# Relative attention on one core: pairs of half heads in another order, with operands loaded in pieces and half of the output inside the loop

## The chip, the cores and the metric

The kernel runs on one core of a Trainium2 chip. The metric is the device time of one execution in microseconds. A core has five engines with an instruction stream each: TensorE (PE; its weight loads are listed as PEld), VectorE (DVE), ScalarE (ACT), GpSimd (POOL) and SyncE (SP), which in this kernel issues every DMA. Instructions of one engine run in order; across engines they wait for semaphores.

## The reference

Two branches over x (16 sequences, 512 positions, 128 features) are added. One is attention with relative positions, 16 heads of 8 features; the other is a feed-forward net with weights of plus or minus one.

```python
xn = (x - mu) / jnp.sqrt(var + 1e-05) * ln_g + ln_b
q = (xn @ Wq + bq).reshape(B, S, H, dh)        # k and v alike
p = (pe @ Wp).reshape(S, H, dh)
content = jnp.einsum('bihd,bjhd->bhij', q + u_bias, k)
pos = _relative_shift(jnp.einsum('bihd,jhd->bhij', q + v_bias, p))
attn = jax.nn.softmax((content + pos) * scale, axis=-1)
head = jnp.einsum('bhij,bjhd->bihd', attn, v).reshape(B, S, Dm)
return head @ Wo + bo                          # the attention branch
...
h = jnp.concatenate([x, -x], axis=-1)
h = s0 * _conn_dense(k0, h)
h = jax.nn.relu(h) * 2
h = s1 * _conn_dense(k1, h)
```

The relative shift makes the position score of row i and column j depend on their distance. The last axis of the scores has 512 columns, so 16 x 16 x 512 rows are normalised.

## The kernel before

**Setup.** Layer norm, projections and the feed-forward branch come first. They leave in DRAM the queries (`qu_scr`, `qv_scr`), keys (`k_scr`), windows of position projections (`p_scr`, `pd_scr`), values (`v_scr`) and the finished residual of both biases and the feed-forward branch (`res_scr`). The first maximum of the attention loop starts 267.95 us after the span's start.

**The loop.** A unit is a group of query rows for one head, over all 16 sequences: 32 units a head, 512 in all. A cycle works on two units, after a fixed list of steps (`STEPS`, yielded by `attention_order`). For a unit, `scores` (L786 to L833) makes the scores in two halves on PE (steps A and B: L797 from the keys, L813 and L826 from the windows), `max_first` (L840, step F) and `max_second` (L845, G and H) reduce over chunks on DVE, `transposed` (L850, T) and `max_over_rows` (L854, N) finish the maximum, and `exponentials` (L859 on PE, L869 on ACT, steps X and Y) writes the exponentials. A pair is 16 units, that is one half of a head's query blocks (`up` 0 or 1): eight cycles. The exponentials of one pair stay in one of two buffers `e_t`, and while the next pair is scored, step V (`weighted`, L887 on PE, L896 copies on ACT) multiplies them with the values; a ninth row of the values gives the denominators. Each of the eight V steps of a pair, k = 0 to 7, makes an eighth of it.

The orders of PE, DVE and ACT are written by hand (`ORDERED`); the order of SP is the scheduler's, until a point near the end from which it is by hand as well. A DMA has to wait for the one eight before it, because eight semaphore lanes are used in turn.

**Loads.** Before, pair n is head n // 2, half n % 2. The keys, windows and values of a head are double-buffered by head (`load_head`, L196 to L208, 13 DMAs), the queries by groups of eight units (`load_queries`, L210 to L228, 12 DMAs of 64 KB), all issued at the second unit of a group.

**Numerators and denominators.** When half of a pair's sums have been copied (`av`), `stored_sums` issues the load of the denominators into a tile of 128x16 (`den`, L921, 8 KB) and four stores of the sums (L926). Later a list of due steps runs at step F of an even unit: the reciprocal (L929) and the store of the inverse (L931); when both halves of a head are there, `divided` loads the numerators (`raw`, L942) and the inverse broadcast to all eight features (`rden`, L943), multiplies on POOL (L946, 128x512) and stores to `head_scr` (L947).

**The tail.** In the last two pairs `last_steps` gathers all heads from `head_scr` into two SBUF tiles `sums` (L960), loads the residual (L970, eight DMAs of 512 KB in all) and divides the last head (L963, L978 on POOL, 8x2048). The last pair's sums are divided in place by `last_sums` (L901 to L909; reciprocal L906, product L907) and moved (L911). Then `output_of` does the output projection for both halves: 64 matmuls (L986), 16 adds of 128x512 (L994) and stores of 256 KB (L997).

Of the kernel before, what the change touches and what calls it, by code (L numbers as in the profile page):

```python
# [44 lines left out]
OTHERS = ((slice(0, L0), slice(0, L0)), (slice(L1, P), slice(L0, P - DH)))  # L45
ORDER = (*OTHERS, (slice(L0, L1), slice(P - DH, P)))
# [41 lines left out]
def rel_attention_and_binary_ffn(  # L88
# [59 lines left out]
    sum_scr = scr("sum_scr", [H - 1, DH, B, 2, 2 * P], F32)  # L148
    rden_scr = scr("rden_scr", [H, B, 2, 2 * P], F32)
    head_scr = scr("head_scr", [P - DH, B, 2, 2 * P], F32)  # L150
# [45 lines left out]
    def load_head(h):  # L196
        m = h % 2
        src = p_scr.rearrange("t (d h) s j -> (t d) h s j", h=H)[:, h]
        src_d = pd_scr.rearrange("t (d h) s n j -> (t d) h s n j", h=H)[:, h]
        for n in range(4):  # L200
            rows_n = slice(32 * n, 32 * n + 32)
            nc.sync.dma_start(
                k_t[m][rows_n], k_scr.rearrange("t (d h) b j -> (t d) h b j", h=H)[:, h, n::4, :]
            )
            nc.sync.dma_start(win[m][rows_n], src[:, :, 3 - n : 3 - n + WIN])
            r, side = n // 2, n % 2
            nc.sync.dma_start(win_d[m][rows_n], src_d[:, side, :, 1 - r : 1 - r + WIND])
        nc.sync.dma_start(v_t[m], v_scr[:, h].rearrange("p b f -> p (b f)"))  # L208

    def load_queries(h, l):  # L210
# [3 lines left out]
        for n in range(4):  # L214
# [15 lines left out]
    with ExitStack() as pre:  # L230
# [515 lines left out]
        stores = [lambda: quads_stored(0), lambda: load_head(0), lambda: load_queries(0, 0)]  # L746
# [35 lines left out]
    with ExitStack() as att:  # L782
        manual = ExitStack()
        manual.enter_context(tc.manual_schedule(engines=ORDERED))
        def scores(n, half, st):

            h, u = st["h"], st["u"]
            sp = st["ps"][half]
            blocks = sp.rearrange("p c a r b -> p (c a) r b")
            kt = k_t[h % 2]  # L790
# [15 lines left out]
            for side, off, dist in ((0, LO_OFF, range(-1, -NC, -1)), (1, UP_OFF, range(1, NC))):  # L806
                for d in dist:
                    cs = [c for c in (2 * half, 2 * half + 1) if 0 <= c - d < NC]
                    if not cs:
# [5 lines left out]
                        lhsT=win[h % 2][:, side, y0 : y0 + P],  # L815
# [8 lines left out]
            for t in range(2):  # L824
# [3 lines left out]
                    lhsT=win_d[h % 2][:, t, UP_OFF - 4 * u : WIND - 4 * u],  # L828
# [9 lines left out]
        def max_first(n, st):  # L838
            st["m"] = wk.tile([P, 2 * P], BF16, tag="m", name=f"m_{n}", bufs=3)
            nc.vector.tensor_reduce(  # L840
                st["m"], flat(st["ps"][0]).rearrange("p c x -> p x c"), AX.X, ALU.max
            )

        def max_second(n, st, c):
            nc.vector.tensor_tensor(st["m"], flat(st["ps"][1])[:, c], st["m"], ALU.max)  # L845

        def transposed(n, st):
            st["pt"] = t_t[:, 0]
            for f in range(2):
                nc.tensor.transpose(st["pt"][:, f, :], st["m"][:, f * P : (f + 1) * P], ident_b)  # L850
# [25 lines left out]
        def weighted(pair, k):  # L876

            h = pair["h"]
# [5 lines left out]
            for r in range(4):  # L884
# [4 lines left out]
                    lhsT=v_t[h % 2][:, v0 : v0 + VW],  # L889
                    rhs=pair["eT"][:, b, c],  # L890
                    start=(c == 0 and (g == 0 or at_end)),
# [8 lines left out]

        def last_sums(pair, half, g):  # L901

            av = pair[half][:, g]
            nc.tensor.matmul(t_bank[:, g], lhsT=sel, rhs=av, start=True, stop=True)  # L904
            inv = sequences(e_t[0], 1, 1)[:, 2 * half + g]
            nc.vector.reciprocal(inv, t_bank[:, g])  # L906
            nc.vector.tensor_tensor(av, av, inv, ALU.mult)  # L907
            if g and half == 0:
                last_moved(pair, half, range(4))  # L909

        def last_moved(pair, half, rs):  # L911
            for r in rs:
                b = 8 * half + 2 * r
                nc.sync.dma_start(sums[1][L0:L1, b : b + 2], pair[half][32 * r : 32 * r + DH])

        def stored_sums(pair, half):
# [6 lines left out]
            for r in range(4):  # L923
                b = 8 * half + 2 * r
                dst = sum_scr[h, :, b : b + 2, up, :] if h < H - 1 else sums[up][L0:L1, b : b + 2]
                nc.sync.dma_start(dst, av[32 * r : 32 * r + DH])  # L926

            def inverted():
                nc.vector.reciprocal(den, den)  # L929
                inv = rden_scr[h, bs, up]  # L930
                nc.sync.dma_start(inv.rearrange("b (q m) -> b q m", q=16), den)  # L931
                if h == H - 1:
                    load_rden(half)
                elif up == 1 and half == 1:
                    divided(h)
# [3 lines left out]
        def divided(h):  # L939

            raw, rden = (wk.tile([P, S], F32, tag=name, name=f"{name}_{h}", bufs=1) for name in ("raw", "rden"))
            nc.sync.dma_start(raw, sum_scr[h].rearrange("w b u i -> (w b) (u i)"))  # L942
            nc.sync.dma_start(  # L943
                rden, rden_scr[h].rearrange("b u i -> b (u i)").unsqueeze(0).to_broadcast([DH, B, S])
            )
            nc.gpsimd.tensor_tensor(raw, raw, rden, ALU.mult)  # L946
            nc.sync.dma_start(head_scr[h * DH : (h + 1) * DH].rearrange("w b u i -> w b (u i)"), raw)  # L947
# [4 lines left out]


        rden, res = [], []

        HB = [slice(0, B // 2), slice(B // 2, B)]

        def load_sums(up, bs):
            for dst, src in OTHERS:
                nc.sync.dma_start(sums[up][dst, bs], head_scr[src, bs, up])  # L960

        def load_rden(half):
            nc.sync.dma_start(  # L963
                rden[0][L0:L1, HB[half]],
                rden_scr[H - 1, HB[half], 0].unsqueeze(0).to_broadcast([DH, B // 2, 2 * P]),
            )

        def load_res(up, bs):
            for m in range(2):
                nc.sync.dma_start(  # L970
                    res[up][64 * m : 64 * m + 64, bs].rearrange("p b k d -> p (b k) d"),
                    half_rows(res_scr, up, m, bs),
                )

        def divide(qs, eng):
            bs = slice(4 * qs[0], 4 * qs[-1] + 4)
            t = sums[0][L0:L1, bs]
            eng.tensor_tensor(t, t, rden[0][L0:L1, bs], ALU.mult)  # L978

        def output_of(up, q):  # L980

            for g in range(2):
                po = s_t[(4 * up + q) % 3][g].rearrange("p c a b r -> p (c a b r)")
                b = 4 * q + 2 * g
                for x in range(4):
                    nc.tensor.matmul(  # L986
                        po[:, x * D : (x + 1) * D],
                        lhsT=sums[up][:, b + x // 2, x % 2 * P : (x % 2 + 1) * P],
                        rhs=wo_sb,
                        start=True,  # L990
                        stop=True,
                    )
                t = res[up][:, b : b + 2].rearrange("p b k d -> p (b k d)")
                nc.vector.tensor_tensor(t, po, t, ALU.add)  # L994
            bs = slice(4 * q, 4 * q + 4)
            for m in range(2):
                nc.sync.dma_start(  # L997
                    half_rows(out, up, m, bs),
                    res[up][64 * m : 64 * m + 64, bs].rearrange("p b k d -> p (b k) d"),
                )  # L1000
# [3 lines left out]
        def sequences(t, half, n):  # L1004

            t = t[:, HB[half]].rearrange("p b c a i -> p (b c a i)")
            return t.rearrange("p (n b i) -> p n b i", n=2, b=B)[:, n]

        def last_steps(n, k):

            free = e_t[0]
            if (n, k) == (0, 2):
                load_sums(0, slice(0, B))
            elif (n, k) == (0, 3):
                sums.append(sequences(free, 0, 0))
                load_sums(1, slice(0, B))
            elif (n, k) == (0, 4):
                res.append(q_t[0].bitcast(F32).rearrange("p b (k d) -> p b k d", k=2))
                load_res(0, HB[0])
                rden.append(sequences(free, 0, 1))  # L1020
            elif (n, k) == (0, 6):
                load_res(0, HB[1])
            elif (n, k) == (0, 7):
                divide((0, 1), nc.gpsimd)
            elif (n, k) == (1, 1):
                res.append(sequences(free, 1, 0).rearrange("p b (k d) -> p b k d", k=2))
                load_res(1, HB[0])
            elif (n, k) == (1, 3):
                load_res(1, HB[1])
                divide((2, 3), nc.gpsimd)  # L1030

        loads = [(h, l) for h in range(H) for l in range(NL)]
        units, pairs, later, due, filled = {}, {}, [], [], []
        quads_stored(2)
        for op, n, *k in attention_order():
            if op == "A":
                h, u = n // NU, n % NU
                if u % UP == 0:
                    pairs[n // UP] = {
                        "n": n // UP,  # L1040
                        "h": h,
                        "up": u // UP,
                        "eT": e_t[n // UP % 2],
                    }
                if n == 2:
                    quads_stored(3)
                units[n] = {"h": h, "u": u, "eT": pairs[n // UP]["eT"], "ps": s_t[n % 3]}
                scores(n, 0, units[n])
                nl = n // UL + 1
                if u % UL == 1 and 2 <= nl < len(loads):  # L1050
                    if nl % NL == 0:
                        load_head(nl // NL)
                    load_queries(*loads[nl])
            elif op == "B":
                scores(n, 1, units[n])
            elif op == "F":
                max_first(n, units[n])
                if due and n % 2 == 0:
                    due.pop()()
# [87 lines left out]
```

## Time and profile before

| | |
|---|---|
| median of three runs | 1376.68 us (1376.38 to 1377.88) |
| the profiled execution | 1373.51 us, span 1371.7 us |
| first maximum of the loop, last one | 267.95 us, 1313.65 us |
| a cycle of two units, as most are | 4.045 us |
| L869 ACT, exponentials, 1024 | 623.7 us, 690 ns each |
| L845 DVE, second maximum, 1024 | 431.6 us, 422 ns each |
| L840 DVE, first maximum, 512 | 348.2 us, 680 ns each |
| L797, L813, L826 PE, scores | 406.7, 342.8 and 227.7 us |
| L946 POOL, division of a head, 15 | 19.1 us, 1273 ns each |
| DMA, all queues | 160.22 MB, share of the 16 engines 43.5% |

How it is read: the page gives busy time and instruction count of each engine, then the span in 40 slices, in which PEclk is TensorE's granted clock in tenths. A group is a line, an engine, an operation and its tiles with shapes, then count, busy time, mean of one in ns, and after the second bar the idle time ahead of it with the instruction that ended most of it. A wait names the engine, the line that waited, and what released it: us in total, times, longest. SPq is the DMA queue of SyncE. A line of the timeline has start, duration, engine, line, operation and tiles. A line of the windows has the stretch, its length, busy time of PE, PEld, DVE, ACT and POOL, then the granted clock, the DMA share and GB/s.

### The profile page before, as it was taken

To read this page: it belongs to the slowest core of one execution; us is meant where nothing else is said; L and a number is where in the kernel's file an instruction comes from. 1 tells how busy PE (TensorE), PEld (TensorE's weight loads), DVE (VectorE), ACT (ScalarE), POOL (GpSimd) and SP (SyncE) were. 2 spreads that over 40 slices of the span, in tenths; PEclk is the share of its full clock that TensorE was granted. 3 is DMA by queue.
4 is the path that set the end of the run, shared out by engine and by line. 5 is a ranking of instruction groups with operands and counts; after the bars stand their busy time and mean duration, and the time that the engine had idled before them with its cause. 6 is when DMAs were issued, how large, how long until landed. Compare 5 with 4: busy or idle time off the path is not lost. (4 is left out here: it accounts for less than half of the span.)

```text
span 1371.7 us, 55178 instructions
## 1 busy us (share of the span) xinstructions
PE 1295.0 (94%) x23061; PEld 970.3 (71%) x23061; DVE 1137.7 (83%) x2723; ACT 832.6 (61%) x1456; POOL 130.8 (10%) x115
## 2 busy tenths in 40 slices
PE   4988889999999999999999999999999999999966
PEld 2555555577778777777877877778777777777744
DVE  8988754688888888888888888888888888888846
ACT  4566668466666666666666666666666666566630
POOL 4333345010000000000000000000000000000011
PEclk9999999999999999999999999999999999999988
DMA  4587869873232333333333323333333253323288
GB/s 117 171 222 192 191 171 257 242 220 92 76 99 74 94 79 95 95 86 86 93 89 83 94 74 97 83 93 84 95 80 99 75 128 84 95 74 88 68 146 190
DMA packets 243606, 160.22 MB, mean 117 GB/s; under 512 B 79510, under 2 KB 227100, under 8 KB 243356
## 3 DMA queue, kind: packets, MB, share of 16 engines
q1 hardware_dynamic: 243356, 156.69, 43.5%
q8 instruction: 181, 2.97, 0.9%
q14 instruction: 69, 0.57, 0.1%
HBM read 96.34 MB, written 59.48 MB: 114 GB/s over the span
## 5 line engine op out<-in xcount | busy, mean ns | idle before, releaser
L869 ACT ACTIVATE e<-s,e_scale 128x512 f32<-128x512 f32 x1024 | 623.7, 690 | 218.2 <-PE s L859 218.1
L845 DVE TENSOR_TENSOR m<-s,m 128x256 bf16<-128x256 f32 x1024 | 431.6, 422 | 112.9 <-PE s L826 77.6
L797 PE MATMUL s<-q,k 128*128 128x64 f16 x8192 | 406.7, 193 | 2.1 <-issue 1.0
L859 PE MATMUL s<-ident_b,nm 128*128 128x256 bf16 x2048 | 383.8, 275 | 7.3 <-DVE nm L854 7.3
L797 PEld LDWEIGHTS <-k 128*128 128x128 f16 x8192 | 358.5, 98 | 23.6 <-issue 2.8
L840 DVE TENSOR_REDUCE m<-s 128x256 bf16<-128x512 f32 x512 | 348.2, 680 | 1.0 <-ACT e L869 0.6
L813 PE MATMUL s<-q,win 128*128 128x128 f16 (+1 forms) x4096 | 342.8, 206 | 0.1
L887 PE MATMUL a_t<-e,v 128*9 128x256 f32 x4032 | 266.0, 381 | 0.6 <-ACT e L869 0.6
L813 PEld LDWEIGHTS <-win 128*128 128x128 f16 x4096 | 231.4, 98 | 0.3 <-issue 0.3
L826 PE MATMUL s<-q,win_d 128*128 128x64 f16 x2048 | 227.7, 193 | 0.0
L854 DVE TENSOR_REDUCE nm<-t_t 128x2 bf16<-128x256 bf16 x512 | 214.7, 419 | 7.1 <-PE t_t L850 2.9
L859 PEld LDWEIGHTS <-nm 128*128 128x128 bf16 x2048 | 131.0, 98 | 117.8 <-DVE m L845 99.0
L896 ACT COPY av<-a_t 128x256 f32<-128x256 f32 x126 | 46.9, 372 | 186.2 <-PE a_t L887 161.2
L887 PEld LDWEIGHTS a_t<-e,v 128*9 128x9 f32 x4032 | 86.4, 90 | 81.2 <-issue 1.6
L850 PE MATMUL t_t<-ident_b,m 128*128 128x128 bf16 x1024 | 141.3, 220 | 1.4 <-DVE m L845 1.3
L826 PEld LDWEIGHTS <-win_d 128*128 128x128 f16 x2048 | 129.8, 98 | 0.0
L946 POOL TENSOR_TENSOR raw<-raw,rden 128x512 f32<-128x512 f32 x15 | 19.1, 1273 | 992.3 <-DMA rden<-rden_scr 992.3
L640 PEld LDWEIGHTS <-e 128*128 128x128 f16 x512 | 49.6, 98 | 59.7 <-issue 12.6
L850 PEld LDWEIGHTS <-m 128*128 128x128 bf16 x1024 | 80.9, 98 | 11.3 <-DVE m L845 4.9
L618 DVE SCALAR_TENSOR_TENSOR h2l<-s,h2h 128x512 f16<-128x512 f32 x45 | 30.9, 686 | 37.6 <-ACT h2h L617 37.4
L640 PE MATMUL s<-h1l,e 128*128 128x512 f16 x180 | 47.2, 379 | 0.5 <-DVE h1l L618 0.4
L640 PE MATMUL s<-h1h,e 128*128 128x512 f16 x180 | 47.2, 384 | 0.3 <-DVE h1l L618 0.2
(176 smaller groups left out, 888.3 us busy)
## 6 DMA issues: line engine op xcount, KB each, us to landing
q<-qv_scr SPq DMA_DIRECT2D x512, 64.0 KB
q<-qu_scr SPq DMA_DIRECT2D x256, 64.0 KB
qu_scr<-k SPq DMA_DIRECT2D x32, 256.0 KB
k_scr<-hv SPq DMA_DIRECT2D x64, 128.0 KB
qu_scr<-win SPq DMA_DIRECT2D x32, 256.0 KB
qv_scr<-e SPq DMA_DIRECT2D x16, 512.0 KB
k<-k_scr SPq DMA_DIRECT2D x64, 128.0 KB
win<-p_scr SPq DMA_DIRECT2D x64, 79.5 KB
```

What stands on the lines that cost most here:

```text
L640: nc.tensor.matmul(ph, lhsT=w[:, t, f * P : (f + 1) * P], rhs=h[t][m], start=(m == 0 and t == 0), stop=(m == 1 and t == n - 1),)
L797: nc.tensor.matmul(sp[:, c % 2, :, :, 4 * g : 4 * g + 4].rearrange("p a r (n m) -> p n (a r) m", m=2), lhsT=kt[:, g, c * P : (c + 1) * P], ...
L813: nc.tensor.matmul(blocks[:, x0 : x0 + (NC + 1) * (len(cs) - 1) + 1 : NC + 1], lhsT=win[h % 2][:, side, y0 : y0 + P], rhs=qp[:, side, :, c ...
L826: nc.tensor.matmul(blocks[:, x0 : x0 + NC + 2 : NC + 1, 2 * t : 2 * t + 2], lhsT=win_d[h % 2][:, t, UP_OFF - 4 * u : WIND - 4 * u], rhs=qd ...
L840: nc.vector.tensor_reduce(st["m"], flat(st["ps"][0]).rearrange("p c x -> p x c"), AX.X, ALU.max)
L845: nc.vector.tensor_tensor(st["m"], flat(st["ps"][1])[:, c], st["m"], ALU.max)
L850: nc.tensor.transpose(st["pt"][:, f, :], st["m"][:, f * P : (f + 1) * P], ident_b)
L854: nc.vector.tensor_reduce(st["nm"], st["pt"], AX.X, ALU.max, negate=True)
L859: nc.tensor.matmul(flat(st["ps"][half])[:, :, f * P : (f + 1) * P], lhsT=st["nm"][:, f : f + 1].to_broadcast([P, P]), rhs=ident_b.unsqueez ...
L869: nc.scalar.activation(st["eT"][:, :, cs, :, i0 : i0 + 4].rearrange("p b c a r -> p (c a) b r"), st["ps"][half].rearrange("p c a r b -> p ...
L887: nc.tensor.matmul(bank[32 * r : 32 * r + VW, g], lhsT=v_t[h % 2][:, v0 : v0 + VW], rhs=pair["eT"][:, b, c], start=(c == 0 and (g == 0 or ...
L896: nc.scalar.copy(pair[half][:, g], bank[:, g])
```

## The change

The pairs are taken with `up` outermost: the first halves of all 16 heads (pairs 0 to 15), then the second halves (16 to 31). So a pair's head changes with every pair, and keys, windows and values are loaded for each pair instead of each head, buffered by the pair's parity. `load_head` and `load_queries` take the piece numbers to load; the pieces are put on a list `loading`, and each unit's step A issues one piece of three DMAs. The values are loaded on their own at the sixth unit.

`divided` works per pair, 128x256 instead of 128x512, and its product goes straight into the SBUF tile `all_sums` one cycle later, or to `early_scr` for the second halves of heads 0 to 4, since their rows are still needed. `head_scr` is gone. All due steps run at each step F of an even unit, and each returns what follows it a cycle later: the reciprocal, then the inverse's store, then `divided`, then its store; the reciprocal itself is due one cycle later than before.

The output of the first halves is made while pairs 17 to 20 are multiplied with their values (step V, while 18 to 21 are scored): `first_output`, one sequence each odd k, two matmuls into the free half of the bank `a_t`, an add of 128x256 on DVE at the next due time, two stores of 64 KB, and the residual of the sequence after the next.

At the end the residual of the second halves is loaded by `load_last` (four DMAs of 512 KB) into the query buffer in pair 30's step k = 3, from where SP's order is by hand. `last_sums` uses the `raw` and `rden` tiles for its inverses. `last_output` does the second halves alone, and its stores go out on SP's and ACT's queues in turn.

```diff
-    def load_head(h):
-        m = h % 2
+    def load_head(h, m, ns=range(4)):
...
+    def load_values(h, m):
         nc.sync.dma_start(v_t[m], v_scr[:, h].rearrange("p b f -> p (b f)"))
-    def load_queries(h, l):
+    def load_queries(h, l, ns=range(4)):
...
         def last_sums(pair, half, g):
-            nc.tensor.matmul(t_bank[:, g], lhsT=sel, rhs=av, start=True, stop=True)
-            inv = sequences(e_t[0], 1, 1)[:, 2 * half + g]
-            nc.vector.reciprocal(inv, t_bank[:, g])
+            dens = t_bank[:, 1]
+            nc.tensor.matmul(dens, lhsT=sel, rhs=av, start=True, stop=True)
+            name = ("raw", "rden")[g]
+            inv = wk.tile([P, 2 * P], F32, tag=name, name=f"{name}_{pair['n']}_{half}", bufs=1)
+            nc.vector.reciprocal(inv, dens)
             nc.vector.tensor_tensor(av, av, inv, ALU.mult)
...
             def inverted():
                 nc.vector.reciprocal(den, den)
+                return inverse_stored() if n == 2 * H - 2 else inverse_stored
+
+            def inverse_stored():
                 inv = rden_scr[h, bs, up]
                 nc.sync.dma_start(inv.rearrange("b (q m) -> b q m", q=16), den)
-                if h == H - 1:
-                    load_rden(half)
-                elif up == 1 and half == 1:
-                    divided(h)
+                if half == 1:
+                    return lambda: divided(pair, slice(0, B))
+                if n == 2 * H - 2:
+                    return lambda: divided(pair, bs)
...
+            nc.sync.dma_start(raw, sum_scr[h, :, bs, up])
+            nc.sync.dma_start(rden, rden_scr[h, bs, up].unsqueeze(0).to_broadcast([DH, nb, 2 * P]))
             nc.gpsimd.tensor_tensor(raw, raw, rden, ALU.mult)
-            nc.sync.dma_start(head_scr[h * DH : (h + 1) * DH].rearrange("w b u i -> w b (u i)"), raw)
+            if up and h < EARLY:
+                dst = early_scr[h * DH : (h + 1) * DH]
+            else:
+                dst = all_sums[rows_of_head(h)]
+
+            def stored():
+                nc.sync.dma_start(dst[:, bs], raw)
...
+        def first_output(b, free):
+            products(a_t[:, free], b)
+            def added():
+                t = first_res.pop(b)
+                nc.vector.tensor_tensor(t, a_t[:, free], t, ALU.add)
+                res_rows(t, 0, b, store=True)
+                load_first(b + 2)
...
+                    (nc.sync, nc.scalar)[m].dma_start(
+                        half_rows(out, 1, m, b),
...
-        loads = [(h, l) for h in range(H) for l in range(NL)]
+        loads = [(h, 2 * up + l) for up in range(2) for h in range(H) for l in range(2)]
...
+                if n % UL == 1 and 2 <= nl < len(loads):
+                    loading += [lambda nl=nl, m=m: load_queries(*loads[nl], [m]) for m in range(4)]
+                if n % UP == 1 and nl + 1 < len(loads):
+                    h1, m1 = loads[nl + 1][0], (n // UP + 1) % 2
+                    loading += [lambda h1=h1, m1=m1, m=m: load_head(h1, m1, [m]) for m in range(4)]
+                if n % UP == 5:
+                    loading.append(lambda h=h, m=n // UP % 2: load_values(h, m))
+                if loading:
+                    loading.pop(0)()
...
-                if due and n % 2 == 0:
-                    due.pop()()
+                if n % 2 == 0:
+                    due = [more for more in (do() for do in due) if more]
...
+                if k == 0 and n == H + 1:
+                    load_first(0)
+                    load_first(1)
+                if k % 2 and H < n < H + 5:
+                    due.append(first_output(4 * (n - H - 1) + k // 2, k // 2 % 2 ^ 1))
+                if k == 1 and n == H + 6:
+                    nc.sync.dma_start(all_sums[: EARLY * DH], early_scr)
+                if n < 2 * H - 2:
+                    if k % 4 == 2 and later:
+                        due.append(later.pop(0))
+                    if k % 4 == 3:
+                        later.append(stored_sums(pair, k // 4))
+                elif k in (2, 4):
+                    due.append(later.pop(0))
+                elif k == 3:
+                    later.append(stored_sums(pair, 0))
+                    load_last()
+                elif k == 6:
+                    last_sums(pair, 1, 0)
```

## The prediction

> **What bounds the kernel now.** I read the page's first two parts, the groups, the waits, the SP queue of one pair, the tail in order of time, and the clock there.
>
> ```profile
> span 1371.7 us, 55178 instructions
> PE 1295.0 (94%) x23061; PEld 970.3 (71%) x23061; DVE 1137.7 (83%) x2723; ACT 832.6 (61%) x1456; POOL 130.8 (10%) x115
> PEclk9999999999999999999999999999999999999988
> ...
> DVE den L929 <- DMA den<-av: 27.7, 13, 17.1
> ...
> SPq L931 <- DVE m L845: 199.3, 47, 6.6
> SPq L947 <- POOL raw L946: 68.1, 15, 5.2
> ```
>
> PE is busy 94% of the span at full clock: inside the loop whatever adds to PE adds to the time. The last three lines are waits (total, times, longest): DVE waits 27.7 us for the denominators' transfer (L929), and the SP queue stands long in two waits for compute.
>
> ```profile
> L986 PE MATMUL s<-wo_sb,sums 128*128 128x128 f32 x64 | 7.6, 277 | 0.0
> L986 PE MATMUL s<-wo_sb,e 128*128 128x128 f32 x64 | 7.3, 275 | 0.0
> L946 POOL TENSOR_TENSOR raw<-raw,rden 128x512 f32<-128x512 f32 x15 | 19.1, 1273 | 992.3 <-DMA rden<-rden_scr 992.3
> ...
> 1036.54 0.43 SPq L208 DMA_DIRECT2D v<-v_scr  x1
> 1037.01 0.62 SPq L943 DMA_DIRECT2D rden<-rden_scr  x1
> 1037.68 0.51 SPq L216 DMA_DIRECT2D q<-qu_scr  x1
> 1038.29 0.37 SPq L220 DMA_DIRECT2D q<-qv_scr  x1
> 1038.76 0.37 SPq L224 DMA_DIRECT2D q<-qv_scr  x1
> 1043.37 0.34 SPq L947 DMA_DIRECT2D head_scr<-raw  x1
> ```
>
> Here the queue issues every 0.47 us, then stands from 1039.1 to 1043.4 until the broadcast inverse has landed and POOL has multiplied.
>
> ```profile
> 1315.20 4.06 SPq L931 DMA_DIRECT2D rden_scr<-den  x1
> 1319.30 1.83 SPq L970 DMA_DIRECT2D q<-res_scr  x1
> 1328.67 0.29 SPq L963 DMA_DIRECT2D e<-rden_scr  x1
> ...
> 1335.75 0.25 DVE L929 RECIPROCAL den<-den 128x16 f32<-128x16 f32 x1 [17.12 <-DMA den<-av]
> ...
> 1328.00:1330.00 2.00, 0.00 (x0) 0.00 (x0) 0.00 (x0) 0.00 (x0) 0.00 (x0) 0.50 0.78 135
> ```
>
> In the tail an 8 KB store issued at 1315.20 frees its reader only at 1328.67, behind large loads; DVE and PE stand, and PE's clock falls to 0.50 (last line, column before the last two). The timeline of the loop gives the cycle: 4.045 us, 32.36 per pair of eight cycles; the last first maximum (L840, cycle 255) starts at 1313.65, so the tail is 58.1 us.
>
> **The change, term by term** (the profiled execution took 1373.51 us, 1371.7 in the span; that is 3.17 under the median of 1376.68, so I sum against 1373.51 and add 3.17).
>
> *Output of the first halves inside the loop.* The two L986 groups are 14.9 us for 32 sequence halves, 0.466 each; 16 of them move out of the tail into the eight-cycle stretches in which pairs 18 to 21 are scored: +7.3 us on PE (0.457 each by the later group). Their 16 adds are 128x256 from PSUM, as L845 (0.422 each): 6.8 us of DVE, which has 17% free, unless PE stands until the PSUM half is read. With every add in PE's way that is 6.8, with none 0; the wait DVE m L845 on PE shows that DVE mostly waits for PE, so I take a third, 2.4. PE's own floor in this stretch: +9.7.
>
> *SP in these four pairs.* Before, the loop's SP issued 1269 DMAs in 617 us of 970; with gaps 0.51 each. After, a pair has 24 q, 13 head, 2 den, 8 sums, 2 inverse stores and one each of raw, rden, store: 52, or 26.5 us of 32.36. Stores and residual loads of the outputs add about 62 (64 less those that fall behind): 31.6. Then the store behind POOL: the 128 KB broadcast lies between 64 KB (2.46 to 2.91 from issue to the next lane's release) and 256 KB (5.03), by size 3.5; POOL half of 1.27, 0.7; less 0.6 issue and three q DMAs (1.4): 2.2 a pair, 8.9 in all (0 to 14). Residual loads that wait for their store: 2. Together 4×26.5+31.6+8.9+2−1.5 (head start that the queue has) = 147 against 139.1 of PE (129.4+9.7). So SP decides: region cost 147−129.4 = **+17.2** (ends: 9.7 if SP keeps up, 22).
>
> By the Trainium skill, "DMA: Bandwidth & Descriptors", Rules for kernel authors, a transfer whose outermost dimension counts under 16, as a leading broadcast of 8, runs on no more engines than that; this speaks against 31 broadcasts in place of 15. The rows agree in part: 256 KB of raw land in 2.8 us, 256 KB of rden in 5.03. By the rule 128 KB on 8 engines would take what 256 KB take on 16, 2.8, and the region would cost some 2.8 less.
>
> *Start.* The second pair's k, win, win_d, v (9 issues × 0.51 = 4.6 us) now stand before its queries: these land at 303.4 to 304.7 by the queue's order, and scores need them at 301.65: **+2.3** (0 to 5, hidden if the setup's waits absorb it).
>
> *One 640 KB load of the first five heads*: before, a 1536 KB load at 1128 landed in 10.5 us and PE stood 1.2: **+1.2** (0 to 2). Residual loads that wait for their setup store: **+0.3**.
>
> *Other pairs.* 52 issues (26.5) plus the waits fit into 32.36; the den load waits for the av copy at 19.5 after the pair's start, and behind it stand sums, the last query group and raw/rden. The last piece lands 30.8 to 31.6, scores need it at 32.4: **+1.5** for the odd hiccup (the queue takes about 1 us for one DMA in 18), bounds 0 to 8. The 20 MB more from HBM are covered: 43.5% DMA share.
>
> *At nothing.* POOL makes 31 multiplications of half the size instead of 15 (0.7 each): it is idle for 992 us ahead of L946. The heads' results go straight into SBUF, so the 1536 KB and 384 KB gathers vanish with the scratch; they were charged where they stalled (1128, tail).
>
> *Denominators a cycle later.* In-loop L929 waits add to 10.05 us, the 1128 gap to 1.2, other stray gaps 0.8: **−12.06** (0 if none goes). DVE then reaches the reciprocal four cycles behind the av copy (before, three: 12.1 us against a den load that is issued up to 8 us late and lands 1.86 after). The inverse's store comes one cycle after its reciprocal, so that SP's 199 us in L931 shrink; behind that wait stand the next query pieces.
>
> *Tail.* Gone: 16 of 32 sequence halves and their 2 MB, the 8x2048 multiplications (4.5 us each). New: the reciprocal of the next to last pair's sums (L916, in cycle 255) uses the tile of the raw numerators, which has one buffer, so DVE must wait until POOL's last multiplication (L962) is done and its store has landed; behind it on DVE stand that cycle's last maxima, and PE, ACT and the last pair wait for those. From the first maximum of cycle 252: den and sums issued until 4.8; four 512 KB residual loads (before, such four landed 12.5 after the first issue) until 17.3; the inverse behind them, 17.5; rden 21.2, POOL 21.95, store landed 24.0 (2.0 as L947); the half pair's raw and rden 27.5, POOL 28.2, landed 30.3. DVE comes there at 14.6 (three cycles and 2.5): it stands 15.7 (13 to 18). PE, cold again, costs 2.9 (1338 to 1341 at 0.50). V of the last pair begins 6.6+15.7+2.9 = 25.2 after the last first maximum; then V 8.2 (128 matmuls, 16 in 1.04), reciprocal and product 2.2 (1.74+0.43), half of an SBUF move of 2.0, products 16 × 0.457 = 7.3 with the adds beside them, the last stores' issue 4.6 (seven at 0.66), landing 3.9: 27.2. Tail 52.4 against 58.1: **−5.7** (−11 with the best of each term, −2 with a stall of 18 and slower landings; −21 with no wait at all). Two more reciprocals of 1.74 than before lie in that stall.
>
> Output stores on a second queue I count as issue time alone. The Trainium skill, same page, Issuing engines are not separate DMA queues, says that this is all it saves; were it more, half of 1 MB at the 226 GB/s of the last slice, some 2 us, would go. No row here has two queues.
>
> Sum: 17.2+2.3+1.2+0.3+1.5−12.06−5.7 = +4.7: 1378.2, and on the median's scale 1381.
>
> **Rivals.**
> - *SP keeps up in the four pairs.* The bound is then PE and the adds. For: SP is 64% busy now, and rden may land in 2.8. Then 9.7 instead of 17.2: −2.8, **1374**. Against: 68 issues a pair are 34.6 us.
> - *The tail's wait is short* (other side). If the inverse is not held behind the 2 MB, L962 is done near 20 and DVE stands 5 or less: −6 or below, **1367**, down to 1362. It is faster than before once that wait is under 8.2 us (15.7 less 4.7 and 2.75). Against: the row at 1315.20, held 13.4 us.
> - *The last query piece is late in every pair*: 1 us × 26 pairs = +26, **1405**. For: margin 0.8 to 1.6; against: before, the queue stood 200 us in L931 with slack.
> - *The den waits do not go*, as the queue reaches the den load late: 10 us stay, **1391**.
>
> **Numbers.** Forecast 40% (own range 1376 to 1387), SP keeps up 22%, short wait 20%, late queries 13%, den waits 5%. A measurement tells about 0.2%, 2.75 us. Faster: the short wait 20, half of SP keeping up 11, a tail of the forecast 1: 0.32. Same: the other 11 and a sixth of the forecast, 7: 0.18. Slower 0.50. The range 1366 to 1396 leaves out the lower half of the short wait and most of the late queries, some 2 in 10.
>
> **What would show it.** Cycles in pairs 18 to 21 of 4.6 us with PE idle for q loads, 4.045 elsewhere; no L939 idle for den in the loop; in the tail one DVE idle of 13 to 18 us ahead of L916, with a clock of 0.5 after it; L1035 adds ending about 8 us before the span. Wrong if the four pairs stay near 4.35 a cycle (PE floor), if L916 waits less than 8 us, or if q is awaited in every pair.

## The result and the profile after

The changed kernel takes 1416.72 us (median of four, 1413.83 to 1419.44) against 1376.53 of the kernel before: a ratio of 1.0291, 95% interval 1.0262 to 1.0321, so 40 us slower. The forecast was 5 us slower, with a range that ended at 1396: right in its sign, far off in its size.

The lines of the page after that answer to those of before:

```profile
span 1415.0 us, 55613 instructions
PE 1311.5 (93%) x23065; PEld 982.2 (69%) x23065; DVE 1141.4 (81%) x2734; ACT 835.9 (59%) x1456; POOL 125.3 (9%) x129
PE   4998989999999999999999999878999999999947
PEclk9999999999999999999999999999999999999978
...
L799 PE MATMUL s<-q,k 128*128 128x64 f16 x8192 | 408.0, 193 | 20.5 <-DMA q<-qv_scr 18.0
L852 PE MATMUL t_t<-ident_b,m 128*128 128x128 bf16 x1024 | 141.5, 220 | 21.2 <-DVE raw L916 20.2
L962 POOL TENSOR_TENSOR raw<-raw,rden 128x256 f32<-128x256 f32 (+1 forms) x31 | 22.6, 727 | 1054.6 <-DMA rden<-rden_scr 948.3
```

The row of PE and the line of the first matmuls before:

```profile
PE   4988889999999999999999999999999999999966
L797 PE MATMUL s<-q,k 128*128 128x64 f16 x8192 | 406.7, 193 | 2.1 <-issue 1.0
```

Three things are to be seen. The row of PE has a dent, 878, at about two thirds of the span, where before there are only nines: that is where the first halves' output is made. The first matmuls of a unit (L799, the same line as L797 before) now wait 18.0 us for a query transfer. And PE once stands 20.2 us behind the reciprocal of L916; that is the tail.

Where the time went is read from the starts of the first maximum of each cycle (L842 after, L840 before), from one profiled execution of each. The excess is over 4.045 us a cycle. The output's stretch is the 32 cycles in which pairs 18 to 21 are scored and the one behind them.

| us | before | after | difference |
|---|---|---|---|
| start of the span to the first maximum | 268.0 | 270.4 | +2.4 |
| excess in the first pair | 2.2 | 2.5 | +0.3 |
| excess in the output's stretch | 2.0 | 43.0 | +41.0 |
| excess in all other cycles | 10.1 | 9.0 | −1.1 |
| last first maximum to the end | 58.1 | 58.7 | +0.6 |
| sum (difference of the spans) | | | +43.2 (+43.3) |

So nearly all of it lies in one stretch, the expected gain of the denominators is not there, and neither is that of the tail. The cycles of pair 21 in that stretch last, in order, 6.62, 4.13, 5.18, 4.13, 5.14, 4.13, 5.18 and 8.98 us; before they are 4.05. Two different things lengthen them. What the engines wait for there, from the waits of after in the window 860 to 1034 (total, times, longest), and below it the same of the SP queue, and the longest wait of that queue in the same window of before:

```profile
PE s L799 <- DMA q<-qv_scr: 17.7, 4, 6.0
PEld a_t L995 <- ACT av L897: 15.3, 15, 1.0
```

```profile
SPq L969 <- POOL raw L962: 8.7, 4, 2.5
SPq L932 <- ACT e L871: 4.3, 5, 2.4
```

```profile
SPq L931 <- DVE m L845: 35.2, 8, 5.6
```

The four long cycles, one at each pair's end, are the first line of the first list: the next pair's queries are not there, and the cycle behind is long with them (6.62 here). The cycles of 5.14 to 5.18 are the second, beside the product's own time: the output's product waits for ACT's copy, once for each sequence. The SP queue in that window waits little, 8.7 us for POOL and some 15 in shorter waits; it has too much to issue. Its timeline in pair 21:

```profile
1018.53 1.33 SPq L984 DMA_DIRECT2D out_dram<-o  x2
1019.91 0.58 SPq L218 DMA_DIRECT2D q<-qu_scr  x1
1020.53 0.45 SPq L222 DMA_DIRECT2D q<-qv_scr  x1
...
1021.56 1.25 SPq L982 DMA_DIRECT2D o<-res_scr  x2
...
1026.56 0.43 SPq L226 DMA_DIRECT2D q<-qv_scr  x1
1028.93 0.34 SPq L969 DMA_DIRECT2D early_scr<-raw  x1
1029.37 1.90 SPq L984 DMA_DIRECT2D out_dram<-o  x2
```

From 986.08 to 1029.37, one pair, the queue issues 68 DMAs, which keep it busy for 37.0 us; the rest is 2 us of waiting for POOL (ahead of 1028.93) and gaps of some 0.07. The two pairs before that are alike: 68 DMAs each, 36.4 and 36.6 us. Most stores and loads of the output cost 0.60 to 0.66 us, a few up to 2.2, and the query load that follows one 0.58 instead of 0.43.

In the tail the DVE's wait came as forecast, longer:

```profile
1363.15 0.60 SPq L944 DMA_DIRECT2D rden_scr<-den  x1
1365.56 0.72 POOL L962 TENSOR_TENSOR raw<-raw,rden 128x256 f32<-128x256 f32 x1 [40.25 <-DMA rden_scr<-den]
1366.31 0.64 SPq L969 DMA_DIRECT2D sums<-raw  x1
...
1373.90 0.72 POOL L962 TENSOR_TENSOR raw<-raw,rden 64x256 f32<-64x256 f32 x1 [7.62 <-DMA rden<-rden_scr]
1374.65 0.66 SPq L969 DMA_DIRECT2D sums<-raw  x1
1377.66 1.76 DVE L916 RECIPROCAL raw<-t_t 128x256 f32<-128x256 f32 x1 [18.83 <-DMA sums<-raw]
```

The window behind it (length, busy time of PE, PEld, DVE, ACT and POOL, then PE's clock):

```profile
1377.60:1382.50 4.90, 2.84 (x26) 1.90 (x27) 3.46 (x5) 1.60 (x3) 0.00 (x0) 0.50 0.00 0
```

DVE stands 18.83 us until the store of POOL's last product has landed, and the clock behind it is 0.50.

### The profile page after: what moved, and what is told of

The parts are those of the page before. It is cut to its first block, busy times and chain, and to the rows that moved or that the text cites. A ratio compares the mean times of both kernels' runs of the same rounds, so it can differ in the third digit from the quotient of the medians.

```text
span 1415.0 us, 55613 instructions
## 1 busy us (share of the span) xinstructions
PE 1311.5 (93%) x23065; PEld 982.2 (69%) x23065; DVE 1141.4 (81%) x2734; ACT 835.9 (59%) x1456; POOL 125.3 (9%) x129
## 4 chain that ended last, share of the span: by engine, by line
PE 69%; DVE 7%; SPq 6%; DMA 5%; ACT 3%; issue 2%; POOL 0%; POOLq 0%; DVEq 0%; ACTq 0%
PE a_t L888 15%; PE s L861 15%; PE s L799 15%; PE s L815 11%; PE s L828 4%; PE t_t L852 4%; DMA q<-qv_scr 2%; PE s L642 2%; SPq L218 1%; DVE m L847 1%; ACT e L871 1%; SPq L222 1%; PE a_t L676 1%; DMA rden_scr<-den 1%; SPq L226 1%
## 5 line engine op out<-in xcount | busy, mean ns | idle before, releaser
L799 PE MATMUL s<-q,k 128*128 128x64 f16 x8192 | 408.0, 193 | 20.5 <-DMA q<-qv_scr 18.0
L799 PEld LDWEIGHTS <-k 128*128 128x128 f16 x8192 | 361.3, 98 | 42.8 <-issue 11.8
L842 DVE TENSOR_REDUCE m<-s 128x256 bf16<-128x512 f32 x512 | 348.4, 680 | 24.4 <-PE s L828 23.6
L852 PE MATMUL t_t<-ident_b,m 128*128 128x128 bf16 x1024 | 141.5, 220 | 21.2 <-DVE raw L916 20.2
L962 POOL TENSOR_TENSOR raw<-raw,rden 128x256 f32<-128x256 f32 (+1 forms) x31 | 22.6, 727 | 1054.6 <-DMA rden<-rden_scr 948.3
L620 DVE SCALAR_TENSOR_TENSOR h2l<-s,h2h 128x512 f16<-128x512 f32 x45 | 30.9, 686 | 37.3 <-ACT h2h L619 37.0
L619 ACT ACTIVATE h2h<-s 128x512 f16<-128x512 f32 x45 | 27.0, 599 | 35.4 <-PE s L642 35.4
```

What stands on the lines that cost most here:

```text
L799: nc.tensor.matmul(sp[:, c % 2, :, :, 4 * g : 4 * g + 4].rearrange("p a r (n m) -> p n (a r) m", m=2), lhsT=kt[:, g, c * P : (c + 1) * P], ...
L842: nc.vector.tensor_reduce(st["max"], flat(st["ps"][0]).rearrange("p c x -> p x c"), AX.X, ALU.max)
L852: nc.tensor.transpose(st["pt"][:, f, :], st["max"][:, f * P : (f + 1) * P], ident_b)
```

## Experiments

Each is the changed kernel with one thing edited, unless said otherwise. Times are given as ratio to the kernel before on the same chip and, so that they can be added, in us of a kernel before of 1376.5; after is +40.1 on that scale.

**What the first halves' output costs.** The lines of the step V that call `load_first` and `first_output` are taken out.

> The first halves' output is left out altogether: its products, adds, residual loads and stores, so those rows of the result are missing. It measures what the whole of it costs inside the loop. In the trace of after, the stretch from the first of its cycles to the last is 43.3 us longer than five pairs of 32.36. If all of that is the output's doing, the time falls by 43 to 44 us, to 1373. If the new pair order and the third more loads slow these pairs too (rival), it falls by less than 35, to over 1382.

Measured: 1382.08 us, ratio 1.002 (0.9994 to 1.0047), +2.8. Leaving the output out takes 37.3 us away (5 more or less), under the 43 expected and over the 35 of the rival; the plain medians differ by 34.6, so the total doesn't decide between them. The stretch does: its excess falls from 43.0 to 0.8 us, so it is explained by the output alone. That the time falls less is due to other cycles: in this execution the first pair has 5.2 us more than in the profile of after and the cycles outside the stretch 5.7, though the order of the work there is the same.

**Its transfers taken away.**

```diff
-                res_rows(t, 0, b, store=True)
-                load_first(b + 2)
+                if b + 2 < B:
+                    first_res[b + 2] = t
+                else:
+                    res_rows(t, 0, b, store=True)
```

> Products and adds of the first halves stay, but the residual is loaded for the first two sequences only and only the last two sums are stored, so most of those rows are missing: 56 DMAs fewer in the SP queue. Theory (SP cannot issue 67 DMAs in the time of a pair): the late query pieces go, some 24 us, and what is left is PE's own part, 16 cycles with 1.1 us more and 16 with 0.08, so the time is 1393. Rival (PE's and DVE's own order makes the cycles long, the queue only follows): the time stays over 1410.

Measured: 1398.15 us, ratio 1.0136 (1.0084 to 1.0189), +18.7: 2 to 5 us over the theory's 1393, and under the rival's 1410. The stretch has 19.7 us of excess instead of 43.0.

**The same transfers on POOL's queue.**

```diff
-                    nc.sync.dma_start(rows_m, half_rows(res_scr, up, m, slice(b, b + 1)))
+                    nc.gpsimd.dma_start(rows_m, half_rows(res_scr, up, m, slice(b, b + 1)))
...
-                    nc.sync.dma_start(half_rows(out, up, m, slice(b, b + 1)), rows_m)
+                    nc.gpsimd.dma_start(half_rows(out, up, m, slice(b, b + 1)), rows_m)
```

> The same transfers, issued from POOL's queue instead of SP's. Theory (issue time on SP is what lacks): as without these transfers, 1393 (1388 to 1398). Rival (the 16 DMA engines or the landing of the transfers are the limit, wherever they are issued): no gain, 1410 to 1420.

Measured: 1395.77 us, ratio 1.0118 (1.0054 to 1.0183), +16.2. Excess in the stretch 19.3. The time is in the theory's range. All transfers are made, from another issuer, and the gain is that of not making them: it was SP's time that lacked, not the DMA engines. Most of that time is issuing; the output's stores also waited on SP for DVE, some 6.5 us in the four pairs, and that wait went with them, which this run doesn't separate. PE's groups in the stretch, first in this kernel, then in after:

```profile
L799 PE MATMUL s<-q,k 128*128 128x64 f16 x1067 | 53.0, 193 | 0.0
...
L995 PE MATMUL a_t<-wo_sb,sums 128*128 128x128 f32 x64 | 11.4, 300 | 8.2 <-ACT av L897 8.2
```

```profile
L799 PE MATMUL s<-q,k 128*128 128x64 f16 x1040 | 53.3, 196 | 17.7 <-DMA q<-qv_scr 17.7
...
L995 PE MATMUL a_t<-wo_sb,sums 128*128 128x128 f32 x60 | 10.7, 300 | 7.7 <-ACT av L897 7.7
```

The wait for queries is gone; the products' wait for ACT, about 8 us, is the same in both. The Trainium skill ("DMA: Bandwidth & Descriptors", Issuing engines are not separate DMA queues) says that issuing from several engines only saves the sequencer's issue time, usually small beside the transfer. The first half agrees with this run. As to the second, one DMA of the output is issued in 0.60 to 0.66 us and lands 2.1 to 2.3 us after the start of its issue, so it is the smaller part here too; but SP issues them one after another, and with 68 a pair moving the output's was worth 24 of the 43 us.

**The products a cycle later.** On top of the last edit, they come ahead of the next V step and write the half that has been copied by then.

```diff
+                if wanted:
+                    due.append(first_output(*wanted.pop()))
                 for m in range(2):
                     weighted(pair, 2 * k + m)
...
-                    due.append(first_output(4 * (n - H - 1) + k // 2, k // 2 % 2 ^ 1))
+                    wanted.append((4 * (n - H - 1) + k // 2, k // 2 % 2))
```

> As with the transfers on POOL's queue, and the two products of a sequence come ahead of the next V step's matmuls instead of behind this one's, into the half that has been copied meanwhile, so that they need not wait for ACT's copy of the same PSUM bank. In after PE stands 0.5 us there and its weight load 1.0, in 16 cycles. Theory: 16 x 0.5 = 8 us less than with the queue alone. Rival (the products' own time is the 1.1 us, fp32 passes included): within 3 us of it.

Measured: 1388.76 us, ratio 1.0089 (1.0055 to 1.0123), +12.3, 3.9 less than the last one, where 8 were expected; the intervals overlap. The trace is clearer (the first pair of this execution has 5.1 us more than the last one's, which hides part of the gain): the stretch's excess falls from 19.3 to 9.0, a cycle of the output lasts 4.55 instead of 5.16, and the group's wait is gone:

```profile
L995 PE MATMUL a_t<-wo_sb,sums 128*128 128x128 f32 x60 | 10.0, 288 | 0.0
```

What is left, 9.0, is some 0.51 us in each of the 15 cycles with products that still lie in the stretch, a little over the 0.457 of the forecast, and 0.1 in each second cycle.

**The kernel before, with the reciprocal one cycle later.** This is one part of the change by itself.

```diff
-                    if k[0] % 4 == 1 and later:
+                    if k[0] % 4 == (2 if n < 28 else 1) and later:
```

> The kernel before, with the reciprocal of the denominators due one cycle later in pairs up to 27, and nothing else of the change. The forecast counted 10 us of waits for the denominators' load as gone. If they lie on the path, the time is 1376.5 - 10 = 1367 (1364 to 1370). Rival: the wait hides one for the next pair's queries, which stand behind the inverse's store in the SP queue, and the time stays within 3 us of 1376.5.

Measured: 1365.54 us, ratio 0.9908 (0.9884 to 0.9933), −12.7. The waits of the loop before, and the reciprocal's group in this kernel's loop:

```profile
DVE den L929 <- DMA den<-av: 10.5, 12, 2.6
```

```profile
L929 DVE RECIPROCAL den<-den 128x16 f32<-128x16 f32 x60 | 14.5, 242 | 0.7 <-DMA den<-av 0.7
```

The wait falls from 10.5 to 0.7 us, and the excess outside the first pair from 12.1 to 3.5, in the two profiles. One shifted step by itself is worth 0.9%.

**The tail: tiles of their own for the inverses**, and, apart from that, **the residual loaded later.**

```diff
-            name = ("raw", "rden")[g]
-            inv = wk.tile([P, 2 * P], F32, tag=name, name=f"{name}_{pair['n']}_{half}", bufs=1)
+            inv = wk.tile([P, 2 * P], F32, tag="o", name=f"inv_{pair['n']}_{half}_{g}")
```

> The inverses of the last pairs get the tiles of the residual in the loop (two buffers, free by then) instead of those of raw and rden, so that DVE need not wait for POOL's last multiplication and its store. In the trace of after DVE stands 18.8 us there. Theory: the stall goes, and with it the cold clock behind it, 2 to 3 us: 1416.7 - 18 = 1399 (1395 to 1402). Rival: the outputs need the heads' rows that POOL's last store writes, which land 21 us after the last first maximum, and most of the gain is lost to that: over 1408.

```diff
                     later.append(stored_sums(pair, 0))
-                    load_last()
...
+                if n == 2 * H - 2 and k == 7:
+                    load_last()
```

> The four residual loads of 512 KB are issued behind the last store of POOL's product instead of ahead of the inverses' stores; the tiles stay shared. Theory (the 8 KB stores and what reads them are held in line behind 2 MB): POOL's last product is done some 18 us after the first maximum of cycle 252 instead of 30, DVE stands 3 to 5 us instead of 18.8, and the time is 1402 (1399 to 1406), if the loads still land ahead of the adds. Rival (the chain of five dependent transfers is slow by itself): DVE stands over 12 us, over 1410.

Measured: 1413.66 us, ratio 1.0279 (1.0231 to 1.0327), and 1417.0 us, ratio 1.0282 (1.0235 to 1.0329): 1.7 and 1.2 us less than after, where 18 and 15 were expected, with intervals of 7 us to either side. By the totals both rivals have won. The traces say otherwise of the tail itself: from the last first maximum to the end it takes 45.3 and 44.3 us instead of 58.7. In the first kernel L915, the reciprocal, has no wait for a store at all; in the second it stands 6.53 us instead of 18.83, where 3 to 5 were expected:

```profile
L915 DVE RECIPROCAL inv<-t_t 128x256 f32<-128x256 f32 x6 | 10.5, 1756 | 12.0 <-PE t_t L913 12.0
```

```profile
1381.04 1.76 DVE L916 RECIPROCAL raw<-t_t 128x256 f32<-128x256 f32 x1 [6.53 <-DMA sums<-raw]
```

So the edits took 13.4 and 14.3 us out of the tail, and the loop of the same executions was longer by 9.7 and 17.3 us than in the profile of after, with its order of DMAs unchanged: PE's waits for query loads (L799) are 24 and 30 us instead of 18, in the output's stretch and, in the second kernel above all, at other pairs' ends. That makes the totals. Why the transfers were later in these executions the runs don't show.

**All of these together** (transfers on POOL's queue, products later, own tiles, late residual).

> Transfers on POOL's queue, products a cycle later, own tiles for the inverses, residual loads later. If the four costs are independent: 1416.7 - 24 - 8 - 20 = 1365, under the kernel before by 12. Rival: the parts overlap (what PE waits for in the loop is late for another reason), over 1376.

Measured: 1371.87 us, ratio 0.997 (0.9943 to 0.9996), −4.1: 7 us above the 1365 of independent costs and 4 under the rival's 1376. Against the kernel with the first two edits alone that is 16.4 us less, and the tail is 43.9 instead of 56.9 us: where the loop is no longer short of SP's time, the tail's gain does reach the total.

**Two pieces with each unit.** `if loading: loading.pop(0)()` is done twice.

> The version with all four mended, and two pieces of loads issued with each unit instead of one. In it the cycles that end a pair are still longer by 7 us in all and the span between the first pair and the last has 12.7 us more than 4.045 a cycle. Theory (the last query piece is issued too late, behind the denominators' load, which waits for a copy): most of the 7 us go, 1365 against 1372, on the scale of a kernel before of 1376.5 to 1377.5. Rival (the pieces are held up by the queue's other waits, and earlier pieces only move them behind the next wait): within 3 us of 1372.

Measured: 1370.42 us, ratio 0.993 (0.9907 to 0.9953), −9.6, 5.5 less than the last one by the ratios, but only 1.5 by the plain medians; the intervals overlap, and by the second figure the rival stands. The profiles speak for part of the theory: the cycles that end a pair have 3.9 us of excess instead of 6.9, though the first pair takes 3.1 more. The pieces were issued too late, and not all of them come in time now.

**The last residual on POOL's queue, at its old place.**

```diff
-                    nc.sync.dma_start(
+                    nc.gpsimd.dma_start(
                         last_res[64 * m : 64 * m + 64, bs]
```

> As the run before, but the last residual loads are back at their place in pair 30's step 3, on POOL's queue instead of SP's. With the loads on SP's queue the moves of the last sums stand behind 2 MB, and ACT's next copy waits 8 us for a buffer that the moves read. Theory (transfers of one queue are held in line, those of another pass): the moves land at once, the tail falls from 44 to some 38 us, so 6 us less than the run before. Rival (the 16 engines are shared, the small transfers are late behind 2 MB on any queue): no gain, tail 43 or more.

Measured: 1365.9 us, ratio 0.99 (0.9875 to 0.9926), −13.8, 4.1 less than the last one with intervals that overlap; tail 38.4 us against 43.7. What ACT waited for in the tail, in the run before this one and not in this:

```profile
ACT av L897 <- DMA sums<-av: 8.2, 1, 8.2
```

The tail's gain is as expected, its reason is not isolated: POOL, with nothing to hold it, issued the loads 18.4 us ahead of the last first maximum, SP in after 7.7 us ahead of it. Whether it is the other queue or the earlier start that let the moves land in time stays open.

**The division's transfers on POOL's queue too.**

```diff
-            nc.sync.dma_start(raw, sum_scr[h, :, bs, up])
-            nc.sync.dma_start(rden, rden_scr[h, bs, up].unsqueeze(0).to_broadcast([DH, nb, 2 * P]))
+            nc.gpsimd.dma_start(raw, sum_scr[h, :, bs, up])
+            nc.gpsimd.dma_start(rden, rden_scr[h, bs, up].unsqueeze(0).to_broadcast([DH, nb, 2 * P]))
...
-                nc.sync.dma_start(dst[:, bs], raw)
+                nc.gpsimd.dma_start(dst[:, bs], raw)
```

> As the run before, and the numerators' and inverses' loads and the product's store are issued by POOL, which multiplies between them; SP then waits for POOL no more (60.7 us in 31 waits in after) and has 93 DMAs fewer. If SP's waits make the query pieces late: what is left of the late cycles goes, 5 us less than the run before. Rival: POOL's queue now stands in order (product, stores of the output, residuals), the outputs' adds come late in the pairs 18 to 21, and these pairs are slower again by over 5 us.

Measured: 1359.66 us, ratio 0.9857 (0.9832 to 0.9881), −19.7. That is 5.9 less than the last one, as expected. The excess of the cycles that end a pair is 0.9 us instead of 2.9, and the stretch of the output stays at 8.9, so its rival is out. This version beats both kernels, by 1.4% and 4.2%. Its longest wait of the SP queue:

```profile
SPq L218 <- PE s L828: 167.5, 39, 7.8
```

SP now waits mostly for the query buffers to come free (L218), which is what a queue ahead of its work looks like; in after its longest sum of waits was for ACT ahead of the denominators' load (L932, 68.3 us).

## Why the prediction was right or wrong

*Output of the first halves inside the loop* (PE floor +9.7): measured 19.3 and 19.7, in the two kernels in which SP is out of the way. The products' own 7.3 was nearly right, as 9.0 with the wait removed shows. The wait was not the one priced: I put 2.4 for PE's wait for DVE's add, which is 0.2 us in a cycle, and did not see that the products stand behind ACT's copy of the bank's other half, 0.5 us on PE and 1.0 on its weight load, 16 times. The built program has that wait, although the two touch different halves.

*SP in these four pairs* (147 us, region +17.2): this step failed most. The forecast's mechanism was right, SP decides, and its 68 DMAs a pair too; the price of the output's own DMAs was the term most mis-sized. A pair took 43.4 us of SP (the mean of three, 898.6 to 1028.9), not the 36.8 of the sum. The 16 DMAs of the output were put at 0.51 each with their gaps and at 15.5 a pair, 7.9 us; they took 0.72 in the mean, the few long ones included, and a gap of 0.06, some 12.4. The other 52 took 28.2 instead of 26.5, gaps included: 0.49 us each, little over the 0.47 of the loop before, but with gaps of 0.06 to the next, so 0.53 there and 0.54 here, not 0.51. The waits, 3 us a pair, were nearly as priced. So one mean was used for all kinds, and the new kind is dearer. The upper end, 22, was no bound: it took only the broadcast's landing as unknown and left the issue time fixed. (147 less 129.4 is 17.6, not 17.2: a slip that changes little.) With 23.7 us of lateness in place of 7.5, and 19.3 in place of 9.7, the region is 43.0 and not 17.2; this is 26 of the 39 us by which the span of after exceeds the forecast's sum, and the other pairs and the tail make some 6 each.

*Denominators a cycle later* (−12.06): right for what it does; alone it is worth 12.7 us by the ratio, 8.6 by the excess in the two profiles, and in after L939 waits for nothing:

```profile
L939 DVE RECIPROCAL den<-den 128x16 f32<-128x16 f32 x59 | 14.3, 243 | 0.0
```

But *Other pairs* (+1.5, 0 to 8) took most of it back: outside the stretch the excess is 9.0 against 10.1, where the kernel before with the later reciprocal has 3.5. Of the 9.0, 5.0 lie in the cycles that end a pair and 1.6 in those behind them. The waits there name a query load for only 1.2 us of PE's idle time and nothing for another 1.5; that the last query pieces are the cause is argued from the runs: with the pieces issued earlier and the division's transfers off SP the 5.0 to 6.9 us of these cycles fall to 0.9. In other executions of the same loop they were 6 to 14 us. The margin of 0.8 to 1.6 us that the forecast gave was the right thing to look at and the price too low for most executions.

*Start* (+2.3): the first maximum came 2.4 later, but the second pair's queries were late by only some 0.3 us. The former is not this step: the kernels that share this setup start the loop between 264.9 and 270.4. Nor is the 0.3 safe: in the eight executions whose loads go out in the same order, after among them, the first pair has 2.5 to 8.7 us of excess, against 2.2 before. *One 640 KB load* (+1.2): it landed in 7.3 us, and no cycle near it is longer than 4.5; nothing.

*Tail* (−5.7): measured +0.6. The wait is the one forecast, at its place, 18.8 us instead of 15.7. Up to POOL's first product the chain was right to 0.1 us (21.3 after the first maximum of cycle 252), in part by luck: the residual loads landed 2 us later than put and the inverse 0.6 later, and the broadcast took 0.8 less. Then the store of the product took 4.1 and 2.9 us to land where I put 2.0 from L947: it goes to eight SBUF partitions now, no longer to DRAM, and throughout the loop lands after 4.25 us (median of 24), while the same product into DRAM takes 1.7 in three cases of five and 3.2 and 3.4 in the others. Another 1.1 us lie between the wait and V of the last pair, and 2.1 between that and the end.

*Rivals.* That SP keeps up was wrong by the most. The one on the other side, a short wait in the tail, did not come about. Queries late in every pair came about in part: outside the stretch half of the cycles that end a pair are longer, by 0.1 to 0.8 us instead of 1. By the rule weighed in the forecast a broadcast to eight would run on eight engines and take as long as twice the bytes on 16, 2.8 us; after shows 3.3 (median of 29 of 128 KB) against 2.2 for raw of the same size. The value by size, 3.5, was the nearer.

## What to carry to other kernels

Before transfers are added to a stretch, price the issuing queue there by kind: the durations of the new DMAs themselves, with the gap behind each and the step from one kind to another, and not one mean of the old ones. If the sum comes near the stretch's time, the queue can decide it, and the error of the price goes into the total in full; move the new transfers to an engine that is idle, which here gave back all 24 us. A tile that is reused for a last step inherits the waits of its first use: look at whose store must land before the new writer may start. And a gain that is shown alone (here 0.9% for one shifted step) can be taken back in company, so the parts of a change are worth running one by one.

## What was unexpected of the hardware

- The store of 128 KB from 128 partitions into eight SBUF partitions lands after 4.25 us, into DRAM after 1.7 in three cases of five, all issued by SP.
- POOL's queue issued the output's 64 transfers at 0.59 us each, and the stretch was no longer than with 56 of them left out (19.3 and 19.7 us of excess).
- Issue time on SP depends on what went before: the first query load behind one of the output's is 0.58 us, the others 0.43.
- The loop of after and of the two kernels with an edited tail has one order of DMAs, and took 9.7 and 17.3 us longer in the profiled executions of the latter. The total varies also where SP has time to spare: the kernel before took 1370.4 to 1385.3 us in 19 executions.
